# A later norm, later sums and a replanned start in a fused scan, attention and feed-forward kernel

## Chip, cores and metric

The kernel runs on one core of a Trainium2 chip. The metric is the device time of one execution in microseconds, from its first to its last instruction. TensorE multiplies matrices into PSUM banks, VectorE (DVE), ScalarE (ACT) and GpSimd (POOL) work elementwise, SyncE (SP) issues transfers. Each engine takes its instructions in the order in which the program issues them, and waits for others by semaphores.

## What is computed

There are 4 images of 4096 positions with 96 channels. The first layer normalises by groups of 3 channels (over all positions of an image) and then by position, projects to value, gate, delta and to A, B and C of 96 x 16 states, and runs a linear recurrence along the positions. The second layer is a linear attention (scores without a softmax) and a feed-forward with values rounded to 8 bits.

```python
xn = layernorm(groupnorm(x)); proj = xn @ W_in + b_in          # value u, gate, delta d, A, B, C
def step(h, ins):                                              # along the positions
    h_new = d * (A_t * h) + d * (B_t * u_t[..., None])
    y = g_t * jnp.sum(C_t * h_new, axis=-1)
    return (h_new, y)
x = x + ys @ W_out + b_out
t = t + attn(ln(t)) @ Wff + bff
t = t + ffn(ln(t))                                             # 96 -> 384 -> 96, rounded to 8 bits
```

## The kernel before

An image is cut into 8 chunks of 512 positions, so there are 32 chunks; the 96 x 16 states of a chunk are 12 tiles of 128 rows. Step k is tile k, and there are 384 of them. A tile takes three projections of three matmuls each (A, B and C), a copy of B on ScalarE, a product of B on GpSimd, a product of A, the scan and a product of C on VectorE. For the tiles in `ON_POOL` the last is a copy on ScalarE and a product on GpSimd instead. Everything else of a chunk is hung on steps by the table `AT`, which counts from the first step of the chunk. The first six tiles, together with the weights and the norms of chunks 0 and 1, are ordered by a list scheduler, `Plan`, that has assumed costs and assumed times at which data land; it decides only the order in which instructions are issued. `calm` is such an assumed time: no GpSimd weight split and no norm of the second chunk is planned before it. `LOOK` is the time within which two jobs count as equally early, so that their rank decides. Each weight is stored as a rounded high part and a remainder ("split"); ScalarE makes the first (`high`) and VectorE or GpSimd the second (`low`).

```python
AT = {

    "load_x": -39, "centre": -25, "scale": -24, "stats": -22, "rstd": -22, "apply": -21,
    "transpose": -14, "affine": -13, "upper": -13, "low": -12, "proj_d": -9, "d_out": -9,
    "proj_u": -9, "du_out": -9, "write": -9, "read": -6, "proj_gate": -3, "gate_out": -1,

    "gather1": 7, "gather2": 11, "gather3": 14,

    "state_sum": 18, "gated": 18, "project_out": 19, "residual": 19, "stats_a": 20,
    "rstd_a": 21, "apply_a": 22, "transpose_a": 33, "keep": 34, "spill": 39, "gram": 24,
    "gram_out": 24, "gram_add": 26,

    "fetch": 21, "attention": 26, "residual_f": 26, "stats_f": 26, "rstd_f": 27, "apply_f": 29,
    "transpose_f": 30, "quant_in": 31, "hidden0": 37, "relu0": 37, "hidden1": 31, "relu1": 33,
    "hidden2": 38, "relu2": 38, "project_f": 40, "round_out": 40, "bias_out": 40, "total": 46,
    "store": 51,

    "sums": -31,
}
ON_POOL = (0, 2, 7, 8)
XBUFS = 15
# ...
    BANKS = {"A": 2, "B": 1, "C": 1, "D": 1, "M": 3}
# ... class LayerNorm
        def rstd(self, shift=True):

            self.r = small.tile([P, J], F32, tag="rstd", name=f"rstd_{self.nm}")
            nc.gpsimd.tensor_scalar(self.r, self.mv[:, :, 1], self.eps, None, ALU.add)
            self.root()
            if not shift:
                return
            self.nmr = small.tile([P, J], F32, tag="nmr", name=f"nmr_{self.nm}")
            nc.gpsimd.tensor_scalar(self.nmr, self.mv[:, :, 0], -1.0, None, ALU.mult)
            nc.gpsimd.tensor_tensor(self.nmr, self.nmr, self.r, ALU.mult)

# ... class Plan: the list scheduler of the start and of the end
                while ready:
                    best = None
                    for n in ready:
                        j = self.jobs[n]
                        t = max(time.get(j["engine"], 0.0), first[n])
                        for b in j["take"]:
                            r = b.split(":")[0]
                            if len(taken[r]) >= self.rings[r]:
                                x = taken[r][-self.rings[r]]
                                t = max(t, back[x] + self.HOP) if x in back else None
                            if t is None:
                                break
                        if t is None:
                            continue
                        key = (t, j["rank"] + bias[n], -tails[n], n)
                        if best is None or t < best[0] - look or (
                            t < best[0] + look and key[1:] < best[1:]
                        ):
                            best = key
                    if best is None:
                        return None
                    t, n = best[0], best[3]
# ... class GroupNorm
        def sums(self, n):
            self.transpose(n, "M", "gx")
            for k, fn in enumerate((AF.Identity, AF.Square)):
                nc.scalar.activation(
                    self.ps, self.ps, fn, bias=self.c if k == 0 else 0.0,
                    accum_out=self.s[:, k, n : n + 1],
                )

        def moments(self):
            t = small.tile([C, 2], F32, tag="gt", name=f"gt_{self.b}", bufs=2)
            nc.vector.tensor_reduce(t, self.s, AX.X, ALU.add)
            nc.vector.tensor_scalar_mul(t, t, 1.0 / L)
            nc.gpsimd.tensor_tensor(self.mv[:, 0:1], t[:, 0:1], self.c, ALU.subtract)
            nc.gpsimd.tensor_tensor(t[:, 0:1], t[:, 0:1], t[:, 0:1], ALU.mult)
            nc.gpsimd.tensor_tensor(self.mv[:, 1:2], t[:, 1:2], t[:, 0:1], ALU.subtract)
# ... def group_norm(b, s0)
        when = [s0 + AT["sums"] + NT * n for n in range(NCH)]
        if b == 1:
            when = [8, 15, 22, 29, 36, 43, 50, 57]
        if b > 1:
            at(when[0] - 7, load_gx, b, 0)
        at(when[0] - 2, make)
        for n in range(NCH):
            if n:
                at(max(when[n] - 7, when[n - 1]), load_gx, b, n)
            at(when[n], call, "sums", n)
        for n, name in ((1, "moments"), (2, "mean"), (4, "root"), (6, "diagonal"), (8, "spread"),
                        (8, "spread_out")):
            at(when[-1] + n, call, name)
# ... class Front
        def centre(self, engine):
            self.t = sb("z", [P, J, C], F32, f"z_{self.nm}")
            engine.tensor_tensor(self.t, xt[self.b, self.i], gn[self.b][0], ALU.subtract)

        def scale(self, engine):
            engine.tensor_tensor(self.t, self.t, gn[self.b][1], ALU.mult)

        def stats(self):
            self.ln.stats(self.t)
        # ...
        def apply(self):
            self.ln.apply(self.t, self.t)

        def transpose(self):
            self.ps = bank("M", [C, TC], f"xnt_ps_{self.nm}")
            for j in range(J):
                nc.tensor.transpose(self.ps[:, j * P : (j + 1) * P], self.t[:, j, :], ident)
# ...
    def front(b, i, s0, f=None):
        if f is None:
            f = Front(b, i)
            plan = [
                ("centre", f.centre, nc.gpsimd), ("scale", f.scale, nc.gpsimd), ("stats", f.stats),
                ("rstd", f.ln.rstd), ("apply", f.apply), ("transpose", f.transpose),
                ("affine", f.affine), ("upper", f.upper), ("low", f.low), ("proj_d", f.proj, 2),
                ("d_out", f.d_out), ("proj_u", f.proj, 0), ("du_out", f.du_out),
                ("write", f.write), ("read", f.read),
            ]
            if (b, i) not in xt:
                plan.insert(0, ("load_x", load_x, b, i))
        else:
            plan = []
        plan += [("proj_gate", f.proj, 1), ("gate_out", f.gate_out)]
        for name, fn, *args in plan:
            at(s0 + AT[name], fn, *args)
# ... class Tile (k: tile and step; 12 tiles make a chunk of 512 positions)
            self.g, self.r = divmod(k, NT)
            self.on_pool = self.r in ON_POOL
        # ...
        def b_proj(self):
            self.b_ps = self.proj("B", w_bac[0])

        def b_copy(self):
            self.bu = sb("bu", [P, TC], F32, f"bu_{self.nm}")
            nc.scalar.activation(self.bu, self.b_ps, AF.Identity, bias=self.bias(0))

        def b_mul(self):
            nc.gpsimd.tensor_tensor(
                self.bu, self.bu, rep[self.b, self.i][:, 1, self.cg], ALU.mult
            )

        def a_proj(self):
            self.a_ps = self.proj("A", w_bac[1])

        def a_mul(self):

            nc.vector.scalar_tensor_tensor(
                self.a_ps, self.a_ps, self.bias(1), rep[self.b, self.i][:, 0, self.cg],
                ALU.add, ALU.mult,
            )

        def scan(self):
            self.h = sb("h", [P, TC], F32, f"h_{self.nm}")
            nc.vector.tensor_tensor_scan(
                self.h, self.a_ps, self.bu,
                0.0 if self.i == 0 else state[self.sh, self.cg], ALU.mult, ALU.add,
            )
        # ...
        def c_mul(self):
            nc.vector.scalar_tensor_tensor(
                self.slot(), self.c_ps, self.bias(2), self.h, ALU.add, ALU.mult
            )

        def c_copy(self):
            self.ch = self.slot()
            nc.scalar.activation(self.ch, self.c_ps, AF.Identity, bias=self.bias(2))

        def c_mul_pool(self):
            nc.gpsimd.tensor_tensor(self.ch, self.ch, self.h, ALU.mult)
# ... tail of a chunk, and its feed-forward
        def gated():
            nc.vector.tensor_tensor(yg[0:C, :], y_ps.pop(g), gate.pop((b, i)), ALU.mult)
        def project_out():
            ps = v["ps"] = bank("B" if phase["end"] else "M", [P, J, C], f"o_ps_{nm}")
            for j in range(J):
                nc.tensor.matmul(
                    ps[:, j, :], lhsT=yg[:, j * P : (j + 1) * P], rhs=w_o, start=True, stop=True
                )
        def residual():
            nc.vector.tensor_tensor(t, v["ps"], t, ALU.add)
        # ... ffn: apply writes xn on ScalarE, transpose turns it on TensorE into a bank of M
    def planned_start():
        plan = Plan({"A": 2, "B": 1, "C": 1, "D": 1, "M": 3, "bu": 5, "h": 3})
        plan.LOOK = 0.6
        job = plan.job
        # ...
        calm = land("calm", 29)
        hd = job("ACT", 0.43, high_dug, after=[land("raw", 11.9)])
        ld = job("POOL", 0.8, low_dug, after=[hd])
        # ...
        for sh in range(NSH):
            plan.rank = 3 * sh - 3
            for k in range(3):
                t = job("ACT", 0.83, high, k, sh, after=[raw[k]])
                if sh < 2:
                    t = job("DVE", 0.8, low, k, sh, nc.vector, after=[t])
                else:
                    plan.rank = 1 if k == 0 else 3 * sh - 3
                    t = job("POOL", 1.3, low, k, sh, nc.gpsimd, after=[t, calm])
                    low_b = t if k == 0 else low_b
                v = w_bac[k][:, :, :, sh * P : (sh + 1) * P]
                w[k, sh] = job("SP", 1.0, split_copies, *(v[:, n] for n in range(3)), after=[t], late=2.4)
        # ...
                if n.on_pool:
                    t = job("ACT", 0.69, n.c_copy, after=[t, low_b if k == NCG else None], free=[c])
                    if k < START - 1:
                        job("POOL", 1.3, n.c_mul_pool, after=[t, s], free=[f"h:{k}"])
                else:
                    job("DVE", 0.75, n.c_mul, after=[t, s], free=[c, f"h:{k}"])
        # ...
        a = job("POOL", 1.0, second.centre, nc.gpsimd, after=[*g, calm])
        a = job("POOL", 1.0, second.scale, nc.gpsimd, after=[a])
        a = job("DVE", 1.1, second.stats, after=[a])
        a = job("POOL", 1.8, second.ln.rstd, after=[a])
        a = job("ACT", 1.55, second.apply, after=[a])
# ... the steps
    for s in range(min(steps), START):
        call(s)
    for s in range(START, K):
        if 0 <= s + 3 < K:
            tiles[s + 3] = Tile(s + 3)
            tiles[s + 3].b_proj()
            tiles[s + 3].b_copy()
        if 0 <= s + 1 < K:
            tiles[s + 1].a_proj()
        if 0 <= s < K:
            tiles[s].c_proj()
        if 0 <= s - 1 < K:
            tiles[s - 1].keep()
        if 0 <= s + 2 < K:
            tiles[s + 2].b_mul()
        if 0 <= s - 1 < K and tiles[s - 1].on_pool:
            tiles[s - 1].c_mul_pool()
        if 0 <= s < K:
            tiles[s].scan()
        if 0 <= s + 1 < K:
            tiles[s + 1].a_mul()
        if 0 <= s < K and not tiles[s].on_pool:
            tiles[s].c_mul()
        call(s)
        if 0 <= s < K and tiles[s].on_pool:
            tiles[s].c_copy()
```

Of the kernel before, what the change touches and what calls it, by code (L numbers as in the profile page):

```python
# [39 lines left out]
# [9 lines that stand above are left out]
# [5 lines left out]
    "hidden2": 38, "relu2": 38, "project_f": 40, "round_out": 40, "bias_out": 40, "total": 46,  # L54
    "store": 51,

    "sums": -31,
}
ON_POOL = (0, 2, 7, 8)
XBUFS = 15  # L60
# [3 lines left out]
def conv_attn_hybrid_kernel(  # L64
# [296 lines left out]
    class LayerNorm:  # L361


        def __init__(self, eps, nm):
            self.eps, self.nm, self.r = eps, nm, None
# [46 lines left out]
    class Plan:  # L412
# [10 lines left out]
        def job(self, engine, cost, fn, *args, after=(), take=(), free=(), late=0.0):  # L423

            j = dict(
                engine=engine, cost=cost, fn=fn, args=args, take=take, free=free, late=late,
                after=[a for a in after if a], tail=None, end=None, rank=self.rank,
            )
            self.jobs.append(j)
            return j  # L430
# [96 lines left out]
    def at(step, fn, *args):  # L527
        steps.setdefault(step, []).append((fn, args))
# [4 lines left out]
    class GroupNorm:  # L533
# [34 lines left out]

        def sums(self, n):
            self.transpose(n, "M", "gx")  # L570
            for k, fn in enumerate((AF.Identity, AF.Square)):
                nc.scalar.activation(
                    self.ps, self.ps, fn, bias=self.c if k == 0 else 0.0,
                    accum_out=self.s[:, k, n : n + 1],
                )
# [51 lines left out]
    def group_norm(b, s0):  # L627
        q = {}

        def make():  # L630
            q["g"] = GroupNorm(b)
            q["g"].first()

        def call(name, *args):
            getattr(q["g"], name)(*args)
# [10 lines that stand above are left out]
            if n:  # L646
                at(max(when[n] - 7, when[n - 1]), load_gx, b, n)
            at(when[n], call, "sums", n)
        for n, name in ((1, "moments"), (2, "mean"), (4, "root"), (6, "diagonal"), (8, "spread"),
                        (8, "spread_out")):  # L650
            at(when[-1] + n, call, name)
# [107 lines left out]
# [12 lines that stand above are left out]
        else:  # L771
            plan = []
        plan += [("proj_gate", f.proj, 1), ("gate_out", f.gate_out)]
        for name, fn, *args in plan:
            at(s0 + AT[name], fn, *args)

    state = {}
    chs = {}
# [1 line left out]
    class Tile:  # L780


        def __init__(self, k):
            self.k = k
            self.g, self.r = divmod(k, NT)
            self.sh, self.cg = divmod(self.r, NCG)
            self.b, self.i = divmod(self.g, NCH)
            self.nm = f"{self.b}_{self.i}_{self.sh}_{self.cg}"
            self.cols = slice(self.sh * P, (self.sh + 1) * P)
            self.on_pool = self.r in ON_POOL  # L790

        def proj(self, tag, wt):
            ps = bank(tag, [P, TC], f"{tag}ps_{self.nm}")
# [418 lines left out]
    START = 6  # L1212
# [2 lines left out]

    def planned_start():
        plan = Plan({"A": 2, "B": 1, "C": 1, "D": 1, "M": 3, "bu": 5, "h": 3})
        plan.LOOK = 0.6
        job = plan.job
        plan.rank = -5  # L1220

        def land(what, time):
            return job(what, time, lambda: None)
# [24 lines left out]
                c = job("DVE", 0.56, first.centre, nc.vector, after=g)  # L1248


        calm = land("calm", 29)
        hd = job("ACT", 0.43, high_dug, after=[land("raw", 11.9)])
        ld = job("POOL", 0.8, low_dug, after=[hd])
        wd = job("SP", 1.0, split_copies, w_dug[:, 0], w_dug[:, 1], w_dug[:, 2], after=[ld], late=2.2)
# [105 lines left out]
        return second  # L1360

    second = planned_start()

    for n, fn in enumerate((weights_attention, weights_ffn1, weights_ffn2, weights_bias)):
        at(NT + 8 + NT * n, fn)
    for b in range(B):
        for i in range(NCH):
            g = b * NCH + i
            s0 = g * NT
            if g:  # L1370
                front(b, i, s0, second if g == 1 else None)
            for sh in range(1, NSH):
                if g < N - 1 or sh == 1:
                    at(s0 + AT[f"gather{sh}"], gather, g, sh)
            at(s0 + NT, tail, b, i)
            s = s0 + NCH * NT
            first = min(24, AT["fetch"])
            at(s + first if b == B - 1 else min(s + first, K - 4), ffn, b, i, s)
        if b + 1 < B:
            group_norm(b + 1, b * NCH * NT)  # L1380
        s = (b + 1) * NCH * NT
        at(s if s == K else s + AT["gram_add"] - NT + 1, attn_matrix, b, s)
# [82 lines left out]
```

## Time and profile before

| | before |
|---|---|
| median of 3 runs | 1202.92 us (1202.42 to 1204.29) |
| profiled span | 1199.1 us |
| instructions | 19211 |
| scan of a tile, VectorE | 384 in all, 1.21 to 1.27 us each |
| product of B, GpSimd | 384, mean 1.342 us |
| product of C, GpSimd | 128, mean 1.348 us |
| copy of B, ScalarE | 384, mean 0.683 us |
| sums of the group norm, ScalarE | 24 times two activations and two reads of the accumulator |
| remainder of a weight: VectorE / GpSimd | 6 of 0.82 us / 6 of 1.22 us |

In the profile, PE is TensorE's matmuls and PEld its weight loads, which overlap them. Busy shares of 40 equal slices are in tenths, 9 being 90% or more. A line of the timeline holds start, duration, engine, source line, operation, output and inputs by name with their shapes, the number of instructions merged, and in brackets the idle time before it with what ended it. A line of waits holds the waiting instruction, what it waited for, the total in us, the number of waits and the longest.

### The profile page before, as it was taken

The page shows a single profiled execution, that of the slowest core. Times are in us where ns is not written, and L with a number is a line of the kernel's source. Part 1 is how long each engine was busy: PE and PEld are TensorE (multiplying, and loading weights), DVE is VectorE, ACT ScalarE, POOL GpSimd, SP SyncE. Part 2 cuts the span into 40 slices and gives each one's busy share as a digit, 9 for nine tenths or more (in the row PEclk, how much of TensorE's full clock was granted, in tenths as well). Part 3 has the DMA queues.
Part 4 walks back from the last instruction along what each step waited for, and adds up shares of the span by engine and source line. Part 5 has one row for each costly group of instructions (what it writes and reads, how often), then busy time and mean ns, then how long its engine had stood idle before and what let it go on. Part 6 is the DMA issues. An engine that isn't in the chain of part 4 may idle for free. (4 is left out here: it accounts for less than half of the span.)

```text
span 1199.1 us, 19211 instructions
## 1 busy us (share of the span) xinstructions
PE 1148.7 (96%) x5899; PEld 876.9 (73%) x5899; DVE 1110.0 (93%) x2091; ACT 817.8 (68%) x1828; POOL 1032.2 (86%) x1178
## 2 busy tenths in 40 slices
PE   7799999999999999999999999999999999999885
PEld 6567777677777777777777777777777777777663
DVE  6789999999999999999999999999999999999865
ACT  5465666565555777777777777777777777776476
POOL 3877888888988898999998899999999999988564
PEclk8989999999999999999999999999999999999987
DMA  7566776877776766776677677677776787667221
GB/s 187 127 127 145 153 162 159 175 156 160 168 162 150 162 156 146 175 175 156 155 158 164 152 176 177 135 160 160 163 174 153 163 181 159 151 146 165 60 74 46
DMA packets 104288, 182.12 MB, mean 152 GB/s; under 512 B 42637, under 2 KB 50769, under 8 KB 104186
## 3 DMA queue, kind: packets, MB, share of 16 engines
q1 hardware_dynamic: 90060, 106.96, 37.0%
q0 software_dynamic: 13536, 73.93, 31.0%
q8 instruction: 46, 0.75, 0.3%
q14 instruction: 56, 0.46, 0.1%
q10 hardware_dynamic: 590, 0.02, 0.0%
HBM read 69.12 MB, written 24.77 MB: 78 GB/s over the span
## 5 line engine op out<-in xcount | busy, mean ns | idle before, releaser
L808 POOL TENSOR_TENSOR bu<-bu,rep 128x512 f32<-128x512 f32 x384 | 512.3, 1342 | 53.6 <-ACT state L834 38.5
L824 DVE TENSOR_TENSOR_SCAN h<-Aps,state,bu 128x512 f32<-128x512 f32 x336 | 426.0, 1268 | 0.6 <-POOL ch L857 0.5
L805 ACT ACTIVATE bu<-Bps,b_bac 128x512 f32<-128x512 f32 x384 | 262.3, 683 | 188.7 <-PE Bps L269 185.9
L817 DVE SCALAR_TENSOR_TENSOR Aps<-Aps,b_bac,rep 128x512 f32<-128x512 f32 x384 | 281.8, 734 | 12.6 <-PE Aps L269 12.6
L269 PE MATMUL Bps<-xs,w 128*128 128x512 f32 x768 | 268.5, 431 | 16.1 <-ACT bu L805 15.6
L269 PE MATMUL Aps<-xs,w 128*128 128x512 f32 x768 | 242.4, 396 | 1.2 <-DVE h L824 1.1
L857 POOL TENSOR_TENSOR ch<-ch,h 128x512 f32<-128x512 f32 x128 | 172.5, 1348 | 14.1 <-ACT ch L854 10.7
L269 PEld LDWEIGHTS Aps<-xs,w 128*128 128x128 f32 x768 | 143.6, 188 | 38.0 <-DVE h L824 3.7
L269 PEld LDWEIGHTS Bps<-xs,w 128*128 128x128 f32 x768 | 126.5, 191 | 61.1 <-ACT bu L805 26.3
L269 PE MATMUL Aps<-xl,w 128*128 128x512 f32 x384 | 151.9, 396 | 0.0
L269 PE MATMUL Bps<-xl,w 128*128 128x512 f32 x384 | 151.8, 395 | 0.0
L269 PE MATMUL Dps<-xs,w 128*128 128x512 f32 x384 | 121.0, 396 | 0.0
L269 PE MATMUL Cps<-xs,w 128*128 128x512 f32 x384 | 120.7, 395 | 0.3 <-ACT ch L854 0.3
L848 DVE SCALAR_TENSOR_TENSOR ch<-Dps,b_bac,h 128x512 f32<-128x512 f32 x160 | 118.6, 741 | 0.8 <-PE Dps L269 0.7
L863 POOL DMA_DIRECT2D ch<-ch x94 | 90.1, 958 | 0.8 <-DMA ch<-ch 0.8
L269 PEld LDWEIGHTS Bps<-xl,w 128*128 128x128 f32 x384 | 72.5, 189 | 17.7
L269 PEld LDWEIGHTS Dps<-xs,w 128*128 128x128 f32 x384 | 72.3, 188 | 17.6
L269 PEld LDWEIGHTS Aps<-xl,w 128*128 128x128 f32 x384 | 72.2, 188 | 17.7
L269 PEld LDWEIGHTS Cps<-xs,w 128*128 128x128 f32 x384 | 71.9, 188 | 17.9 <-ACT ch L854 0.4
L854 ACT ACTIVATE ch<-Cps,b_bac 128x512 f32<-128x512 f32 x96 | 65.8, 685 | 22.9 <-PE Cps L269 22.9
L269 PE MATMUL Dps<-xl,w 128*128 128x512 f32 x192 | 75.8, 395 | 0.0
L269 PE MATMUL Cps<-xl,w 128*128 128x512 f32 x192 | 75.7, 394 | 0.0
(200 smaller groups left out, 2048.2 us busy)
## 6 DMA issues: line engine op xcount, KB each, us to landing
ch<-ch POOLq DMA_DIRECT2D x94, 768.0 KB, 6.6
rep<-ddd SPq DMA_DIRECT2D x124, 384.0 KB, 7.0
ddd<-dd SPq DMA_DIRECT2D x31, 384.0 KB, 3.2
xl<-lo SPq DMA_DIRECT2D x62, 128.0 KB, 2.5
x<-in_x_dram SPq DMA_DIRECT2D x32, 192.0 KB, 2.9
xatd<-xat SPq DMA_DIRECT2D x32, 192.0 KB, 3.6
xal<-xatd SPq DMA_DIRECT2D x32, 192.0 KB, 2.9
out_dram<-o SPq DMA_DIRECT2D x32, 192.0 KB, 2.1
```

Of the source, the lines that this page charges most:

```text
L269: nc.tensor.matmul(ps, lhsT=wt[:, n], rhs=mv, start=(n == 0), stop=(n == 2))
L805: nc.scalar.activation(self.bu, self.b_ps, AF.Identity, bias=self.bias(0))
L808: nc.gpsimd.tensor_tensor(self.bu, self.bu, rep[self.b, self.i][:, 1, self.cg], ALU.mult)
L817: nc.vector.scalar_tensor_tensor(self.a_ps, self.a_ps, self.bias(1), rep[self.b, self.i][:, 0, self.cg], ALU.add, ALU.mult,)
L824: nc.vector.tensor_tensor_scan(self.h, self.a_ps, self.bu, 0.0 if self.i == 0 else state[self.sh, self.cg], ALU.mult, ALU.add,)
L848: nc.vector.scalar_tensor_tensor(self.slot(), self.c_ps, self.bias(2), self.h, ALU.add, ALU.mult)
L854: nc.scalar.activation(self.ch, self.c_ps, AF.Identity, bias=self.bias(2))
L857: nc.gpsimd.tensor_tensor(self.ch, self.ch, self.h, ALU.mult)
L863: nc.gpsimd.dma_start(chs[g, 0], chs.pop((g, sh)), accum_op=ALU.add)
```

## The change

The norm of the third chunk (`centre`, `scale`, `stats`, `rstd`, `apply`) would by its table be due at steps -1 to 3, which the planned start covers; all of these are issued in one lump between the planned part and step 6. The change puts them at steps 6, 6, 7, 8 and 9. The group norm's sums on ScalarE are issued one step after the transposes on TensorE that they read; before, both were issued at the same step. In the planned part, GpSimd's weight splits and the second chunk's norm may be placed from the assumed time 22 on instead of 29; tiles 0 and 2 multiply C on VectorE and not on ScalarE and GpSimd; and `LOOK` falls from 0.6 to 0.3, so that ranks decide between fewer jobs. No arithmetic changes. The purpose is that no engine waits, in issue order, for something that another delivers late.

```diff
--- before.py
+++ after.py
@@ -54,7 +54,7 @@
     "hidden2": 38, "relu2": 38, "project_f": 40, "round_out": 40, "bias_out": 40, "total": 46,
     "store": 51,
 
-    "sums": -31,
+    "sums": -31, "sums_out": -30,
 }
 ON_POOL = (0, 2, 7, 8)
 XBUFS = 15
@@ -568,6 +568,8 @@
 
         def sums(self, n):
             self.transpose(n, "M", "gx")
+
+        def sums_out(self, n):
             for k, fn in enumerate((AF.Identity, AF.Square)):
                 nc.scalar.activation(
                     self.ps, self.ps, fn, bias=self.c if k == 0 else 0.0,
@@ -646,6 +648,7 @@
             if n:
                 at(max(when[n] - 7, when[n - 1]), load_gx, b, n)
             at(when[n], call, "sums", n)
+            at(when[n] + AT["sums_out"] - AT["sums"], call, "sums_out", n)
         for n, name in ((1, "moments"), (2, "mean"), (4, "root"), (6, "diagonal"), (8, "spread"),
                         (8, "spread_out")):
             at(when[-1] + n, call, name)
@@ -771,8 +774,11 @@
         else:
             plan = []
         plan += [("proj_gate", f.proj, 1), ("gate_out", f.gate_out)]
+
+        late = {"centre": 0, "scale": 0, "stats": 1, "rstd": 2, "apply": 3}
         for name, fn, *args in plan:
-            at(s0 + AT[name], fn, *args)
+            step = s0 + AT[name]
+            at(max(step, START + late[name]) if name in late else step, fn, *args)
 
     state = {}
     chs = {}
@@ -787,7 +793,7 @@
             self.b, self.i = divmod(self.g, NCH)
             self.nm = f"{self.b}_{self.i}_{self.sh}_{self.cg}"
             self.cols = slice(self.sh * P, (self.sh + 1) * P)
-            self.on_pool = self.r in ON_POOL
+            self.on_pool = self.r in ON_POOL and self.k >= START
 
         def proj(self, tag, wt):
             ps = bank(tag, [P, TC], f"{tag}ps_{self.nm}")
@@ -1215,7 +1221,7 @@
 
     def planned_start():
         plan = Plan({"A": 2, "B": 1, "C": 1, "D": 1, "M": 3, "bu": 5, "h": 3})
-        plan.LOOK = 0.6
+        plan.LOOK = 0.3
         job = plan.job
         plan.rank = -5
 
@@ -1248,7 +1254,7 @@
                 c = job("DVE", 0.56, first.centre, nc.vector, after=g)
 
 
-        calm = land("calm", 29)
+        calm = land("calm", 22)
         hd = job("ACT", 0.43, high_dug, after=[land("raw", 11.9)])
         ld = job("POOL", 0.8, low_dug, after=[hd])
         wd = job("SP", 1.0, split_copies, w_dug[:, 0], w_dug[:, 1], w_dug[:, 2], after=[ld], late=2.2)
```

## Prediction

> **What bounds the kernel now.** I read the page first: busy shares, then the 40 slices.
>
> ```profile
> PE 1148.7 (96%) x5899; PEld 876.9 (73%) x5899; DVE 1110.0 (93%) x2091; ACT 817.8 (68%) x1828; POOL 1032.2 (86%) x1178
> ...
> DVE  6789999999999999999999999999999999999865
> ...
> PEclk8989999999999999999999999999999999999987
> ```
>
> VectorE and TensorE are both near full from slice 5 on, so the bulk moves only where one of them waits. The loss lies at both ends. The end (from about 1120 us) is untouched; the start is what four of the five edits concern. Next, busy time by stretch:
>
> ```profile
> 30.00:40.00 10.00, 9.84 (x42) 7.36 (x41) 8.53 (x18) 6.09 (x11) 7.73 (x11) 1.00 0.44 107
> 40.00:50.00 10.00, 8.53 (x36) 5.57 (x35) 6.39 (x9) 6.43 (x15) 10.00 (x10) 1.00 0.45 94
> 50.00:60.00 10.00, 4.05 (x19) 2.75 (x17) 6.67 (x16) 1.23 (x3) 8.62 (x11) 0.82 0.78 179
> 60.00:80.00 20.00, 18.37 (x72) 14.24 (x73) 14.30 (x17) 12.61 (x31) 15.74 (x15) 0.84 0.61 123
> ```
>
> The columns are length, then PE, weight load, DVE, ACT, POOL, clock, DMA share, GB/s. From 40 to 50 us GpSimd is full while VectorE has 6.39 of 10; from 50 to 60 us ScalarE works 1.23 us and TensorE 4.05. The timelines of single engines name the cause:
>
> ```profile
> 54.34 1.03 POOL L667 TENSOR_TENSOR z<-x,gmr 128x384 f32<-128x384 f32 x1
> ...
> 59.46 1.54 ACT L396 ACTIVATE z<-z,nmr_c,rstd_c 128x96 f32<-128x96 f32 x4 [8.13 <-POOL nmr_c L384]
> ...
> 61.63 1.22 PE L269 MATMUL Bps<-xs,w 128*128 128x512 f32 x2 [7.44 <-ACT bu L805]
> ...
> 64.59 0.76 DVE L817 SCALAR_TENSOR_TENSOR Aps<-Aps,b_bac,rep 128x512 f32<-128x512 f32 x1 [3.58 <-PE Aps L269]
> ```
>
> This is one chain. The third chunk's norm belongs to steps -1 to 3, but those are all issued straight after the planned start. GpSimd reaches its `centre` only at 54.34, behind the last weight split (52.03, 2.38 us). ScalarE's `apply` stands behind it in order and idles 8.13 us; the B copies behind that cannot empty the only B bank; TensorE idles 7.44 us; VectorE waits 3.33 us before the stats (56.47) and 3.58 us before tile 8's A (64.59).
>
> The second loss is in the steady part, seen in waits of 400 to 760 us and in the timeline at one such step:
>
> ```profile
> DVE yg L910 <- PE y_ps L872: 8.9, 10, 1.4
> DVE x L920 <- PE o_ps L915: 8.9, 10, 1.0
> ...
> 600.09 0.65 ACT L572 ACTIVATE gx_ps<-gx_ps,gmc 96x512 f32<-96x512 f32 x1 [1.13 <-PE gx_ps L543]
> ...
> 601.48 1.53 ACT L396 ACTIVATE xn<-x,nmr_f,rstd_f 128x96 fp8e5<-128x96 f32 x4
> ...
> 602.00 1.30 PE L1085 MATMUL xq_ps<-ident,xn 128*128 128x128 fp8e5 x4
> ...
> 604.37 0.69 DVE L910 TENSOR_TENSOR yg<-y_ps,gate 96x512 f32<-96x512 f32 x1 [1.13 <-PE y_ps L872]
> ```
>
> `sums` is issued at its own transposes' step. ScalarE, early, waits 1.13 us for them, then works 1.49 us (600.09 to 601.58); the feed-forward's `apply` comes after and ends at 603.0. TensorE reaches that chunk's transposes at 602.0 and holds for them: 1.30 us against 0.40 in the same place at 811.39, where no sums run. The state sum is behind it, and VectorE waits 1.13 us. The starts of `yg` give the price by group of 12 steps: 34.9 us while sums and feed-forward run together (534.71, 569.59, 604.37), 33.5 us after the last sums (947.86, 981.34, 1014.82).
>
> **What the Trainium skill says.** "PSUM — Partial Sum Buffer", section "Engine vs sequencer instructions", has the ScalarE, VectorE and GpSimd queues as strict FIFO. The trace agrees: `apply` and the B copies behind it sit out 8.13 us. "TensorE: Matmul & The Clock Gate", section "What's actually happening", says the clock falls to half after about 3.4 us of idling. It agrees here: after the 7.44 us gap the three A matmuls from 63.08 to 64.36 come 0.43 us apart, against 0.23 for the B matmuls from 32.77 to 33.47. "SBUF — State Buffer", section "SBUF: two separate sides", says a GpSimd operation and a VectorE one with two SBUF inputs lock each other out of a shared port pair. That bears on the earlier GpSimd splits. The trace before doesn't show it: the VectorE split at 28.29, under a GpSimd product, takes 0.83 us, one at 18.87, beside GpSimd's small root, 0.80.
>
> **The change part by part.**
>
> *Third chunk's norm to steps 6 to 9.* It removes the chain above and no work. VectorE's idle time from 53.1 us (end of tile 5's C product) to the start of tile 12's scan at 77.2 is 3.33 + 3.58 + 0.95 + 0.43 + 0.48 = 8.8 us. The later three belong to the slow clock and to catching up. Not all of it returns. GpSimd's steps 6 to 9 now hold four B products (4 x 1.29), centre and scale (2.0), rstd with its shift (1.7), C products of tiles 7 and 8 (2.6) and one gather (1.0), 12.5 us in four steps of some 2.9; ScalarE's step 9 has B copy 0.7, apply 1.54, gate 0.68, sums 1.5, together 4.4 us. I leave 2.5 us of idling there: 8.8 - 2.5 = **6.3 us gained**.
>
> *Calm at 22 instead of 29.* GpSimd idles 8.35 us before 28.88. The six late splits (1.22 us each, 7.3 us) run from 39.96 to 54.41. ScalarE has rounded ten of the twelve pieces by 26.2, so I expect three to five splits in that hole, 3.7 to 6.1 us off the full stretch. *Planned tiles 0 and 2 off GpSimd* takes two products of 1.29 us from it and two copies of 0.69 us from ScalarE, and puts two of 0.75 us on VectorE. *LOOK 0.3* only reorders nearly equal jobs; I count it as zero. VectorE is busy 21.4 of the 26.9 us from 26.16 to 53.1 now and would be 22.9 after; its gaps there (0.43, 0.62, 0.71, 1.05, 0.48, 1.85 and small ones) make 5.5 us. If 1.7 of these go, the 1.5 added are just repaid: **0.2 us**. The splits matter mainly because GpSimd then arrives on time at step 6.
>
> *Sums a step later.* The same 24 transposes and 48 activations. In the event at 600 us, `apply` would start at 598.96 and end at 600.5, before TensorE's 602.0; the transposes take 0.4 and all after moves up by 0.9. The sums land behind tile 9's B copy, at about 601.5 to 603.0, where ScalarE now waits 1.55 us for B (before 605.22). So the wait at `yg` goes, and the one at `x` stays near 0.9, because the 0.35 us of extra transposes remain in TensorE's stream. Ten such waits from 400 to 760 us sum to 8.9 us; two are longer than 0.9 (1.13 and 1.37) and keep a little: **8.3 us**. The other 14 events nearly all lack a feed-forward: the `yg` waits of 200 to 400 us are 0.4 us in all and VectorE is 39.8 of 40 us busy from 240 to 320, so **0.5 us** at most. Against it, `moments` now comes in the same step as the last sums. It may wait up to 0.5 us, three times; I take **-0.5 us**.
>
> Sum: 6.3 + 0.2 + 8.3 + 0.5 - 0.5 = 14.8 us. 1202.9 - 14.8 = **1188 us**.
>
> **Rivals.** (a) ScalarE is only 68% busy, so its wait at the sums, 25.3 us in 23 cases, is hidden and moving it gives nothing: about 1196. Against it speak the 1.30 us transposes and 34.9 against 33.5 us. For it: in groups without feed-forward it is hidden. (b) The wait returns a step later: sums of 1.5 us in front of the next B copy hold the only B bank, or the M bank kept a step longer stops `project_out`. TensorE takes three M banks in order: after the sums come the transposes, the state sum, then a hidden projection at 606.53, 3.5 us after I have the sums ending. I think half the gain is the most this can take: 1192. (c) The start is bound by more than the norm: crowded steps 6 to 10 and VectorE's two added products give back most of it, and only 2 us of 6.5 remain: 1192.5. VectorE's 14.30 of 20 us from 60 to 80 speaks against so little. (d) Early splits on GpSimd run into VectorE's own six splits or delay tile 0's product: some 1 us lost at 28 to 31 us, 1189. (e) Both parts give fully, with the 2.5 us that I left idle, and the planned part is shorter by 3 us because GpSimd no longer paces it: 1182.5.
>
> **Range and chances.** (a) and (c) together, 1201, would need both readings false; (e) is possible. I give 1181 to 1196 eight chances in ten. Faster by over 2% means under 1178.9, 9 us more than my sum, and no idle time that I found pays for it: 0.05. Slower by over 2% would need a new stall of 24 us: 0.01. Within 2%: 0.94.
>
> **What would show it.** Right: no TensorE gap over 3 us between 50 and 65 us; clock 1.0 there; tile 12's scan at about 71 instead of 77.2; GpSimd splits between 22 and 29 us; the wait of the sums on their transposes nearly gone from 25.3 us; `yg` waits from 400 to 760 us under 2 us; groups with sums and feed-forward at 34.0 us, those without still 33.5. Wrong: a wait of B matmuls on `bu` copies or of `o_ps` or `h_ps` on the sums at each sums step; ScalarE waiting over 2 us for `nmr_c` at step 9; a VectorE gap before `moments`; or the first scans later than before, which a different planned order could bring.

## The result, and the profile after

| kernel | median us | against before, 95% interval | gain us |
|---|---|---|---|
| before | 1202.67 | | |
| changed | 1183.57 (1181.53 to 1184.49) | 0.9836 [0.9819, 0.9853] | 19.7 |

The gain here and below is one minus the ratio, times 1202.7 us. The predicted time was 1188, the range 1181 to 1196.

Busy share of TensorE and VectorE, and TensorE's clock, in 40 slices of the changed kernel:

```profile
PE   5999999999999999999999999999999999999885
...
DVE  6999999899999999999999999999999999999865
...
PEclk8999999899999999999999999999999999999989
```

The weak second slice of before (PE 7, DVE 7) is full. The first slice is emptier than before (TensorE 5 instead of 7), and there is one new dent, the eighth slice: clock 8, VectorE 8. By stretch (columns as before: length, PE, weight load, DVE, ACT, POOL, clock, DMA share, GB/s):

```profile
40.00:50.00 10.00, 9.73 (x43) 7.13 (x42) 9.03 (x11) 5.06 (x11) 7.32 (x6) 1.00 0.55 126
50.00:60.00 10.00, 9.85 (x47) 7.58 (x47) 9.90 (x20) 5.76 (x13) 7.68 (x7) 1.00 0.74 173
60.00:80.00 20.00, 19.11 (x86) 14.70 (x85) 18.82 (x31) 13.21 (x32) 18.78 (x23) 1.00 0.75 157
```

From 50 to 60 us TensorE has 9.85 instead of 4.05, VectorE 9.90 instead of 6.67. GpSimd is no longer full from 40 to 50 us. The chain of the third norm in the changed kernel, on ScalarE, TensorE and VectorE (tile 12's scan):

```profile
62.32 1.54 ACT L396 ACTIVATE z<-z,nmr_c,rstd_c 128x96 f32<-128x96 f32 x4 [1.09 <-POOL nmr_c L384]
...
65.87 0.73 PE L269 MATMUL Bps<-xs,w 128*128 128x512 f32 x2 [0.89 <-ACT bu L811]
...
68.94 1.28 DVE L830 TENSOR_TENSOR_SCAN h<-Aps,state,bu 128x512 f32<-128x512 f32 x1
```

and the same scan before:

```profile
77.16 1.27 DVE L824 TENSOR_TENSOR_SCAN h<-Aps,state,bu 128x512 f32<-128x512 f32 x1
```

The timelines of ScalarE, TensorE and VectorE at a sums step of the changed kernel, the one that answers to 600 us before:

```profile
586.56 1.54 ACT L396 ACTIVATE xn<-x,nmr_f,rstd_f 128x96 fp8e5<-128x96 f32 x4
...
589.10 0.65 ACT L574 ACTIVATE gx_ps<-gx_ps,gmc 96x512 f32<-96x512 f32 x1
...
591.97 0.69 ACT L811 ACTIVATE bu<-Bps,b_bac 128x512 f32<-128x512 f32 x1 [1.37 <-PE Bps L269]
...
589.64 0.40 PE L1091 MATMUL xq_ps<-ident,xn 128*128 128x128 fp8e5 x4
...
591.11 0.69 DVE L916 TENSOR_TENSOR yg<-y_ps,gate 96x512 f32<-96x512 f32 x1 [0.18 <-PE y_ps L878]
```

The feed-forward's `apply` now runs ahead of the sums and is done at 588.1, the transposes behind it take 0.40 instead of 1.30 us, and the state sum makes VectorE wait 0.18 instead of 1.13 us. The sums find their transposes done (no wait in brackets; that wait, 25.3 us in the whole trace before, is gone), and ScalarE still idles 1.37 us after them. VectorE's waits from 400 to 760 us:

```profile
DVE x L926 <- PE o_ps L921: 8.4, 10, 1.0
DVE Aps L823 <- PE Aps L269: 1.7, 4, 0.5
DVE yg L916 <- PE y_ps L878: 0.6, 2, 0.4
```

`yg` fell from 8.9 to 0.6 us; `x` stayed. The starts of `yg` give the lead of the changed kernel's trace over that of before, at before's times: 8.8 us at 96, 10.7 at 130, 6.7 at 231, 6.7 at 359, 16.8 at 780, 16.8 at 1131. The two traces are of executions of 1200.81 and 1184.49 us, one below and one above its median, so this lead is 2 to 3 us short of the gain in the table.

### The profile page after: what moved, and what is told of

It reads as the page before. It is cut to its first block, busy times and chain, and to the rows that moved or that the text cites. A ratio compares the mean times of both kernels' runs of the same rounds, so it can differ in the third digit from the quotient of the medians.

```text
span 1182.8 us, 19203 instructions
## 1 busy us (share of the span) xinstructions
PE 1140.1 (96%) x5899; PEld 874.6 (74%) x5899; DVE 1113.2 (94%) x2093; ACT 817.3 (69%) x1826; POOL 1030.3 (87%) x1176
```

## Experiments

Unless another is named, the edit is to the kernel before; the kernels of one table share their runs of before.

**Each part alone.** *Sums a step later only:*

```diff
-    "sums": -31,
+    "sums": -31, "sums_out": -30,
+            at(when[n] + AT["sums_out"] - AT["sums"], call, "sums_out", n)
```

> The kernel before with the sums a step later and nothing else. Theory Q (each wait is a matter of issue order and pays by itself): the lead of the changed kernel grew from 6.7 us at 359 us to 16.8 us at 780 us, so 9 to 11 us faster than before: about 1192 to 1194 us; waits of yg gone from 400 to 760 us, groups with sums and feed-forward at 34.0 us. Theory H (ScalarE's wait at the sums is hidden): 1202 us.

*Third norm later only:*

```diff
+            at(max(step, START + late[name]) if name in late else step, fn, *args)
```

> The kernel before with the third chunk's norm at steps 6 to 9 and nothing else. Theory Q: 5 to 7 us faster, 1196 to 1198 us, TensorE's gap of 7.4 us gone. Theory R (GpSimd, full with weight splits and products until 54 us, is what paces the start; the norm only stands at the end of that queue): 2 to 3 us, about 1200 us, tile 6 to 8 still late for their B products.

*Planned start only:*

```diff
-        plan.LOOK = 0.6
+        plan.LOOK = 0.3
-        calm = land("calm", 29)
+        calm = land("calm", 22)
-            self.on_pool = self.r in ON_POOL
+            self.on_pool = self.r in ON_POOL and self.k >= START
```

> The kernel before with the three planned edits (earlier splits, tiles 0 and 2 on VectorE, LOOK 0.3) and nothing else. Theory Q: the lump of the third norm still stops ScalarE, only a few us earlier, and the first scan is later as in the changed kernel (34.7 against 31.1 us): 0 to 3 us faster, 1200 to 1203 us. Theory R: 6 us or more, 1196 us or less.

*To the changed kernel, calm back:*

```diff
-        calm = land("calm", 22)
+        calm = land("calm", 29)
```

> The changed kernel with the assumed time of calm back at 29. Theory Q: the apply of the first chunk on VectorE is back from 3.31 to about 1.05 us and the first scan earlier by 3 us, against which GpSimd's splits come late again: 1182 to 1187 us. Theory R: early splits are what paid, so 5 us or more of the gain are lost: 1188 us or more.

| kernel | median us | ratio to before | gain us |
|---|---|---|---|
| sums only | 1190.03 | 0.9895 [0.988, 0.991] | 12.6 |
| third norm only | 1197.15 | 0.9955 [0.9942, 0.9968] | 5.4 |
| planned start only | 1197.66 | 0.9967 [0.9954, 0.9979] | 4.0 |
| changed, calm 29 | 1183.72 | 0.984 [0.9821, 0.9859] | 19.2 |

The sums bring 12.6 us (10.8 to 14.4 by the interval), at or above the upper end of the first theory, and the theory that their wait is hidden falls. The third norm alone lands where the theory of issue order put it, but not cleanly: TensorE's gap of 7.4 us is gone and another has come. The timeline of TensorE in that kernel:

```profile
65.24 0.79 PE L269 MATMUL Dps<-xl,w 128*128 128x512 f32 x1 [4.00 <-DMA w<-w]
```

A C product (its bank is D here) waits for the transfer of a weight that GpSimd split last. That split was done at 54.29 us, 11 us earlier, so GpSimd is only part of the delay. SyncE's timeline of that kernel shows where the transfer stood:

```profile
53.87 1.99 SPq L751 DMA_DIRECT2D rep<-ddd  x4
55.90 0.60 SPq L262 DMA_DIRECT2D w<-w  x1
56.54 0.61 SPq L263 DMA_DIRECT2D w<-w  x1
```

It was issued behind four `rep` transfers of 384 KB each, at 56.54, and the matmul started 8.7 us later; the transfers of `w` that this trace times landed in 2.2 to 3.0 us. In every profiled kernel that has the planned edits, or two of the three, the last weights are issued ahead of `rep`, and none has this wait. That is again a matter of order in a queue, though no run here moves these transfers alone. The planned edits alone bring 4.0 us, between the two theories, although the third norm still stands in one lump. And `calm`, on which the rival rested, makes no difference that can be told. Why not is seen on VectorE and GpSimd of the changed kernel:

```profile
21.12 3.31 DVE L403 TENSOR_SCALAR z<-z,mv_c,rstd_c 128x96 f32<-128x96 f32 x4 [0.17 <-POOL rstd_c L392]
24.35 2.47 DVE L259 TENSOR_TENSOR w<-raw,w 128x384 fp32r<-128x384 f32 x2
...
34.74 1.22 DVE L830 TENSOR_TENSOR_SCAN h<-Aps,bu 128x512 f32<-128x512 f32 x1 [0.49 <-POOL bu L814]
...
21.03 1.03 POOL L670 TENSOR_TENSOR z<-x,gmr 128x384 f32<-128x384 f32 x1
22.14 1.08 POOL L673 TENSOR_TENSOR z<-z,gmr 128x384 f32<-128x384 f32 x1
23.18 2.31 POOL L259 TENSOR_TENSOR w<-raw,w 128x384 fp32r<-128x384 f32 x2
```

and of the one with calm 29, where GpSimd is silent from 21.4 to 29.45:

```profile
21.45 1.05 DVE L403 TENSOR_SCALAR z<-z,mv_c,rstd_c 128x96 f32<-128x96 f32 x4 [0.18 <-POOL rstd_c L392]
22.41 1.54 DVE L259 TENSOR_TENSOR w<-raw,w 128x384 fp32r<-128x384 f32 x2
...
31.54 1.22 DVE L830 TENSOR_TENSOR_SCAN h<-Aps,bu 128x512 f32<-128x512 f32 x1
```

Beside GpSimd, the same four operations of `apply` take 3.31 instead of 1.05 us and two splits 2.47 instead of 1.54, 3.2 us on the way to the first scan, which starts 3.2 us later. At tile 12 the changed kernel is still 1.6 us behind this one, by 130 us it is level: `calm` at 22 gives back later what it takes here.

**What of the planned edits counts, and two corrections.** All are edits to the changed kernel. *LOOK back at 0.6:*

```diff
-        plan.LOOK = 0.3
+        plan.LOOK = 0.6
```

> The changed kernel with LOOK back at 0.6 (other edits kept). If LOOK only reorders nearly equal jobs, as predicted: within 1.5 us of the changed kernel, 1182 to 1185 us. Rival: LOOK 0.3 is what brought the late weights in time, and the wait of C matmuls on a weight transfer seen with the norm alone (4.0 us) comes back: 1186 us or more.

*Tiles 0 and 2 on GpSimd again:*

```diff
-            self.on_pool = self.r in ON_POOL and self.k >= START
+            self.on_pool = self.r in ON_POOL
```

> The changed kernel with tiles 0 and 2 multiplying C on ScalarE and GpSimd again. By the prediction's term (two products of 1.29 us off GpSimd against 1.5 us more on VectorE) within 1.5 us of the changed kernel, 1182 to 1185 us. Rival: GpSimd paces 35 to 52 us, so 2.6 us are lost: 1186 us.

*Step 63 relieved:*

```diff
-        at(when[0] - 2, make)
+        at(when[0] - (3 if b == 2 else 2), make)
-            at(when[-1] + n, call, name)
+            at(when[-1] + n + (b == 1 and name == "diagonal"), call, name)
```

> The changed kernel with the second image's first pass of the group norm (transposes and sum of its first chunk, for the third image) at step 62 instead of 63 and the diagonal of the first such norm at 64 instead of 63. In the changed kernel, ScalarE has d's copy, the apply, both diagonals and that first sum at step 63, and the B copy behind them leaves TensorE idle for 2.56 us at 213 to 215.6, after which its clock shows 0.50 for 4 us. If that jam is real: gap under 1 us, period of that group 33 to 36 instead of 40.1 us, 2 to 4 us faster than the changed kernel, 1179.5 to 1182 us. If the jam only moves a step: no faster than 1183 us.

*GpSimd held until the first apply is done* (`lows` are its weight splits):

```diff
+        def hold():
+            nc.gpsimd.tensor_copy(small.tile([P, 1], F32, tag="hold", name="hold", bufs=1), first.t[:, J - 1, 0:1])
+        hold_j = job("POOL", 0.1, hold, after=[a])
+        for j in lows:
+            j["after"].append(hold_j)
-        a = job("POOL", 1.0, second.centre, nc.gpsimd, after=[*g, calm])
+        a = job("POOL", 1.0, second.centre, nc.gpsimd, after=[*g, calm, hold_j])
```

> The changed kernel with GpSimd's second centre and its weight splits held until the first chunk's apply on VectorE is done (a copy of one column of its result on GpSimd, 0.1 us, in front of them). Theory P (VectorE's apply takes 3.31 instead of 1.05 us because GpSimd's operations beside it keep it out): apply back at about 1.05 us, first scan at 32 to 33 instead of 34.7 us, 1.5 to 2.5 us faster than the changed kernel. Rival: the apply is slow for another reason (transfers of weights): still over 2.5 us, and no gain.

| kernel | median us | ratio to before | gain us |
|---|---|---|---|
| changed, LOOK 0.6 | 1186.34 | 0.9868 [0.9852, 0.9885] | 15.9 |
| changed, tiles 0 and 2 on GpSimd | 1182.17 | 0.9834 [0.9819, 0.9849] | 20.0 |
| changed, step 63 relieved | 1179.75 | 0.981 [0.9796, 0.9825] | 22.9 |
| changed, GpSimd held | 1180.9 | 0.9819 [0.9804, 0.9835] | 21.8 |

Tiles 0 and 2 make no difference that can be told. LOOK seems to: 15.9 against 19.7 us, with intervals that just touch. It isn't for the reason that the rival gave; the wait for weights did not come back. VectorE's timeline of that kernel shows three weight splits between the first `apply` and the first chunk's remainder, where the changed kernel has two, and its first scan starts 2.8 us later still, at 37.53:

```profile
23.06 3.20 DVE L259 TENSOR_TENSOR w<-raw,w 128x384 fp32r<-128x384 f32 x3
```

By tile 12 its scan is 2.6 us behind the changed kernel's (71.59 against 68.94). The rest of the 3.8 us the trace can't show: its execution took 1183.27 us, the shortest of four, the others 1186.2 to 1186.5. No run here moves that split alone.

Holding GpSimd shows the conflict. VectorE's timeline of the held kernel:

```profile
21.37 1.05 DVE L403 TENSOR_SCALAR z<-z,mv_c,rstd_c 128x96 f32<-128x96 f32 x4 [0.18 <-POOL rstd_c L392]
...
33.34 1.23 DVE L830 TENSOR_TENSOR_SCAN h<-Aps,bu 128x512 f32<-128x512 f32 x1 [1.28 <-POOL bu L814]
```

Its `apply` is back at 1.05 us and the two splits behind it at 1.52, but the first scan, at 33.34, is only 1.4 us earlier and later than I expected (32 to 33): it now waits 1.28 us for tile 0's B product, before which GpSimd has its three delayed splits (4.49 us) and the second chunk's norm. By 96 us this kernel leads the changed one by 1.6 us. The intervals of the two whole kernels overlap, so the time alone would not prove it; the durations of `apply` do.

The relieved step 63 answers to the dent in the eighth slice. In the changed kernel TensorE's timeline and clock there read:

```profile
215.61 1.22 PE L269 MATMUL Bps<-xs,w 128*128 128x512 f32 x2 [2.56 <-ACT bu L811]
```

```profile
212.00:216.00 4.00, 1.44 (x6) 0.91 (x5) 3.47 (x4) 3.54 (x11) 4.00 (x5) 0.87 1.01 227
216.00:220.00 4.00, 4.00 (x11) 3.13 (x11) 1.06 (x3) 0.77 (x2) 2.57 (x3) 0.50 0.70 185
```

ScalarE is full (3.54 of 4 us) while TensorE has 1.44; then TensorE runs at half clock until about 221.8. That chunk's 12 steps took 40.1 us there, 36.6 in the kernel before with much the same gap (2.7 us) but no clock loss, and 35.8 with the step relieved, where the gap is 1.16 us and not under 1 as expected. Eleven of the profiled kernels have this gap, of 2.35 to 2.81 us. Three show the half clock behind it (the changed one, calm 29, and sums and third norm below: 40.1, 38.6 and 38.5 us for the chunk), eight don't (36.4 to 37.2). So of the 4.3 us between 40.1 and 35.8 about 3 are the clock, lost in some executions and not in others, and about 1.2 the gap. In the time the relief is worth 3.2 us, with intervals that overlap a little.

**Both corrections, and the parts in pairs.** The first joins the two corrections above; the others are the kernel before with two of the three parts.

> The changed kernel with both corrections: GpSimd held until the first apply is done, and the crowded step 63 spread over 62 to 64. If the two are independent, their gains over the changed kernel (2 to 2.7 and 3.8 us) add: about 1177 to 1178.5 us. If the held kernel's clock had merely been luckier at the crowded step, the sum is smaller: 1179.5 us.

> The kernel before with the later sums and the later norm, and its planned start unchanged. If the two parts are independent: 12.6 + 5.4 = 18 us faster, 1184 to 1186 us, with the 4 us wait of C matmuls on a late weight transfer still there; the planned edits then bring only 1 to 2 us on top. If the planned edits are what makes the later norm pay: 1188 us or more.

> The kernel before with the later sums and the three planned edits, and the third norm in its old place. If independent of the norm: 12.6 + 4 to 5 = 17 us faster, 1185 to 1187 us, with the TensorE gap before step 7 at about 3 us. If the norm's place carries the start: 1190 us, no better than the sums alone.

| kernel | median us | ratio to before | gain us |
|---|---|---|---|
| changed, held and relieved | 1177.53 | 0.9794 [0.9779, 0.9808] | 24.8 |
| sums and third norm | 1186.14 | 0.9865 [0.9849, 0.9882] | 16.2 |
| sums and planned start | 1187.16 | 0.9876 [0.9861, 0.9891] | 14.9 |

With both corrections the gain over the changed kernel is 5.1 us, close to 3.2 + 2.1, as expected of independent ones. Its interval lies below the changed kernel's, and overlaps a little with those of the single corrections. The pairs make a table that nearly closes: on top of the sums (12.6) the norm brings 3.6 and the planned start 2.3; on top of both others the norm brings 4.8 and the planned start 3.5. The start's two parts together bring 19.7 - 12.6 = 7.1 us, less than 5.4 + 4.0, but each gain is known to some 1.5 to 2 us only, so they may as well add. In the pair of sums and norm, TensorE waits 4.11 us for the late weight; in the pair of sums and planned start it has the old gap, now 3.49 us at 60 us, and half clock after it (1.22 us for two matmuls). In all three parts together neither is there.

## Why the prediction was right, and where not

The time lay in the range, 4.4 us below the 1188 us of the sum, and the reasons held in kind. Nearly all of the difference is in the sums: 12.6 us where I had 8.3 + 0.5 - 0.5. One of my signs of being wrong did appear, a later first scan (34.74 against 31.08 us), and the rest of the start more than repaid it.

*Third norm: the chain was read rightly, its size nearly.* All of it went: ScalarE waits 1.09 us for the third norm's `nmr_c` instead of 8.13, TensorE has no gap over 0.9 us there instead of 7.44, tile 12's scan starts at 68.94 instead of 77.16; I had said about 71. The idle time that I left in steps 6 to 9 for the crowd is smaller: 1.09 us on ScalarE and 1.04 on VectorE. But "8.8 - 2.5 = 6.3" credited the norm alone with it. Alone it brings 5.4 us and runs into the weight transfer. I had said "the splits matter mainly because GpSimd then arrives on time at step 6"; what the runs show of the planned part is that the last weights go out ahead of `rep`, in time for their matmuls, which I had not looked for. It is so with `calm` back at 29 as well as with LOOK back at 0.6, so neither alone is the cure.

*Planned part: 0.2 us said, some 3.5 measured on top of the other two.* The step that failed is "LOOK 0.3 only reorders nearly equal jobs; I count it as zero": it is the one planned edit whose lack costs, 3.8 us by the times and 2.6 at tile 12 by the traces. Of the early splits I said three to five in the hole before 28.9 us; three are there, and `calm` is worth nothing that can be told in the end, because what rival (d) had at "some 1 us" costs 3.2 us before the first scan. Tiles 0 and 2 are the wash that I had computed. The port rule of the Trainium skill, "SBUF — State Buffer", section "SBUF: two separate sides", was the right thing to have read, but the trace before could not have shown it where I looked: the split at 28.29 was over at 29.12, and the product that I put above it began only at 28.88. I ought to have asked what VectorE does at 21 us, where the earlier work would land. That page also names `tensor_scalar` among the operations that can take a two-port mode, in "Who interferes with whom". The four of `apply` are such (one SBUF tensor, two scalars per partition), and they suffered most: 2.3 of the 3.2 us, beside the second chunk's `centre` and `scale` and the first split. The start as a whole: 6.5 us predicted, 7.1 measured, which is in part luck, since the norm's term was too large and the planned one too small.

*Sums: the mechanism right, one term mis-sized.* For the ten `yg` waits I had 8.3 us; they fell by 8.9 - 0.6 = 8.3. But the lead grew by 16.8 - 6.7 = 10.1 us from 359 to 780 us of the trace before, a longer stretch: in it VectorE's waits at `yg` fell from 9.1 to 0.6 and those at `x` from 10.4 to 9.3 us. One of the latter is the first chunk with a feed-forward (0.91 to 0.29). Groups with sums and feed-forward mostly take 33.8 to 34.5 us where I said 34.0, those without still 33.5. The step that failed is "The other 14 events nearly all lack a feed-forward", with its 0.5 us at most. The sums during the first image come every 7 steps and not every 12, and one of them stands in front of the attention's `apply`. ScalarE, TensorE and VectorE of the kernel before:

```profile
107.19 0.65 ACT L572 ACTIVATE gx_ps<-gx_ps,gmc 96x512 f32<-96x512 f32 x1 [1.51 <-PE gx_ps L543]
...
108.58 1.53 ACT L396 ACTIVATE xa<-x,nmr_a,rstd_a 128x96 f32<-128x96 f32 x4
...
110.74 0.73 PE L269 MATMUL Bps<-xs,w 128*128 128x512 f32 x2 [1.54 <-ACT bu L805]
...
112.45 0.76 DVE L817 SCALAR_TENSOR_TENSOR Aps<-Aps,b_bac,rep 128x512 f32<-128x512 f32 x1 [1.21 <-PE Aps L269]
```

It is the start's chain in small: sums, `apply`, B copy, the only B bank, TensorE, VectorE. With the sums alone moved, TensorE's gap there is 0.47 us, and the chunk takes 1.9 us less:

```profile
109.06 0.73 PE L269 MATMUL Bps<-xs,w 128*128 128x512 f32 x2 [0.47 <-ACT bu L808]
```

By the trace of that kernel some 1.4 us came before 96 us, another 1.9 by 130, 1.0 was lost again by 231 (step 63), and 10.1 came after: 12.4 us together, beside 1.2 us by which its first scan happened to start earlier. The 0.5 us for `moments` was not there: its first operation on VectorE waits for nothing.

Of the rivals, (a) and (b) fell, and (c) was too dark. (d) was real, though mostly in `apply`, which it did not name: three times my size at the first scan, 1.6 us at tile 12, and 2.1 us in the time by the held kernel. (e) came nearest in number, by luck: it put 12 us on the start, which brought 7.1, and 8.3 on the sums, which brought 12.6.

## What to carry to other kernels

An engine that works in issue order and has time to spare still sets the pace when an instruction that waits stands in front of one that others need; look for the waits of such an engine whose next instruction feeds a single buffer. Search every place where a moved instruction stands, not the one that shows it best: here the same sums stood before the feed-forward's `apply` in one stretch and before the attention's in another. The order of transfers in one queue deserves the same look. A part moved alone can uncover a stall that another part removes (the late weight); its trace shows that, while its time, here near what it brings beside the rest, does not.

## What the runs showed of the hardware

- Four VectorE operations of 128x96 with one SBUF tensor and two scalars per partition took 1.05 us with GpSimd silent and 3.31 us beside GpSimd's operations of 1.0 to 1.2 us; subtractions of two SBUF tensors took 0.77 and 1.23 us each. GpSimd's own hardly changed there (1.03 and 1.01 us for `centre`), but in the held kernel, beside VectorE's splits, it paid too: 1.57 us for `centre` and 4.49 for three splits.
- Of eleven TensorE gaps of 2.35 to 2.81 us at the same step, one in each trace, three (2.36, 2.37 and 2.56 us) were followed by half clock, up to some 6.8 us of it, and eight were not, the two longest among them. Five longer gaps near 60 us (3.49 twice, 4.00, 4.11 and 7.44 us) all were. The Trainium skill, "TensorE: Matmul & The Clock Gate", section "What's actually happening", gives about 3.4 us of idling in a window that runs freely; that gaps of one length sometimes cost the clock fits the free window, while 2.36 us is less than the page has.
